# Building the last attention's position bias in the first expert layer's exchange, and writing the attentions' zeros with ScalarE

## The chip, the cores and the metric

The kernel runs on 1 core of one Trainium2 chip. The metric is the device time of one execution in microseconds. The kernel before takes 3750.92 us (median of 3 runs, 3750.13 to 3759.38).

## What is computed

The reference is a stack of four blocks on x of 16 x 64 x 256 (16 sequences of 64 tokens), with a context of 16 x 1601 x 256. Each block is x = x + cross-attention to the context, x = x + self-attention, x = x + feed-forward, each on a layer-normed x. Three pieces matter here.

The last self-attention adds a bias that depends only on the distance of query and key and on the head; nothing in it depends on x:

```python
rel_pos = pos[None, :] - pos[:, None]
buckets = _relative_position_bucket(rel_pos)          # 64 x 64, values 0..31
rel_bias = rel_emb[buckets].transpose(2, 0, 1)[None]  # rel_emb is 32 x 16
att = jnp.einsum('bhqd,bhkd->bhqk', q, k) * (1.0 / math.sqrt(D)) + rel_bias
att = jnp.where(causal[None, None], att, -jnp.inf)
y = jnp.einsum('bhqk,bhkd->bhqd', jax.nn.softmax(att, axis=-1), v)
```

The second block's self-attention is of the same kind without bias and mask. The first block's feed-forward is a mixture of 8 experts: each token goes to 2 of them, each expert takes at most 160 tokens.

## The kernel before

**Order of the work.** x stays in SBUF as 8 tiles of 128 tokens. The stages run one after the other: the first block's attentions (l0_xattn, l0_attn), its experts (l0_ffn), and so on to l3_xattn and l3_attn; l1_attn and l3_attn both call token_attention. The pools decide which memory a tile gets; a tile whose memory belonged to another waits until every use of that other one is over, a DMA's too. The order on each engine follows the program where a helper pins it: mm and tr (L2465, L2470) pin TensorE's, and a Written wrapper (L59) pins what it issues for its engine. Elsewhere the order is the scheduler's. Each engine works strictly in its own order, so an instruction that waits holds all behind it on that engine.

**l0_attn and the exchange.** l0_attn works on two halves a and b of x (4 tiles each). Its last layer's feed-forward for b is feed_last, interleaved with route for each pair of tiles. route (L807 among its lines) computes the gate, ranks the experts, finds with two matmuls (pos) the place of each token in its expert's list, makes put and get from it, and lets GpSimd scatter the tokens to the DRAM tensor taken by four indirect DMAs per pair. route(b, 1) is the last. Then l0_ffn reads the lists back (xs and xw, L947 and L950, on SP's queue, behind the last scatter), TensorE transposes them, VectorE and ScalarE copy the transposes to xsT (L127, L129), and TensorE runs the experts (hidden, out); results go to the DRAM tensor given, and GpSimd gathers them from there (got, L1077). softmax_small (L401 to L406) on the gate's logits, and rms and rr for the next stage (L1095 to L1098), are small VectorE and ScalarE steps that the scheduler puts on VectorE between route(b, 1) and the xsT copies. The tile h1T0, a's hidden layer of l0_attn, is last read by feed's second product for a.

**l3_attn.** It loads its weights, then emb (the 32 x 16 embeddings, four copies on 4 x 32 partitions) and hot (one-hot buckets, 1 MB) by eight DMAs on SP's queue (L2209, L2210). 64 matmuls pb <- emb, hot, which the trace counts as 128, pick the bias (L2215), and 32 VectorE additions (L2225) add the causal mask and lay it out as bias, 128 x 1024.

**token_attention.** Before anything else it makes ones and bq. linear(i) works on half i of the tokens: xln of four tiles on VectorE (L158), transposes on TensorE, two copies to xT, four products of 512 columns (lin_t) of which the first two go to qb by VectorE and ScalarE (L2539, L2540) and the next two to kT, then four products to vm (L2553). Two PSUM buffers serve these products. vm (128 x 4096) holds each value twice, with zeros for the other heads; in linear(0) GpSimd fills it with zeros (L2527). GpSimd also adds the output bias to x there (L2531).

Of the kernel before, what the change touches and what calls it, by code (L numbers as in the profile page):

```python
# [12 lines left out]
F32 = mybir.dt.float32  # L13
I32 = mybir.dt.int32
BF16 = mybir.dt.bfloat16
AF = mybir.ActivationFunctionType
ALU = mybir.AluOpType
# [3 lines left out]
P = 128  # L21
B, S, D = 16, 64, 256
T = B * S
NT = T // P
KC = D // P
# [3 lines left out]
H = 16  # L29
# [35 lines left out]
class Sections:  # L65
# [370 lines left out]
    def l0_attn(self):  # L436
        nc, tc, d = self.nc, self.tc, self.d
# [22 lines left out]
        with ExitStack() as ctx:  # L460
            sb = ctx.enter_context(tc.tile_pool(name="l0a", bufs=1, side="right", reuse_waits="tile"))
            sb2 = ctx.enter_context(tc.tile_pool(name="l0a2", bufs=2, side="right", reuse_waits="tile"))
            ps_kv = ctx.enter_context(tc.tile_pool(name="l0a_kv", bufs=1, space=PSUM, reuse_waits="tile"))
            ps = ctx.enter_context(tc.tile_pool(name="l0a_ps", bufs=1, space=PSUM, reuse_waits="tile"))
            V, A, G = (Written(tc, e) for e in (nc.vector, nc.scalar, nc.gpsimd))
            pieces = self.context_squares(sb2, A)

            def squares(n):
                for _ in range(n):
                    next(pieces, None)  # L470
# [19 lines left out]
            def measure(s, src, p):  # L490

                mv = sb.tile([P, 2, 2], F32, tag=f"ln_mv{s.i}", name="ln_mv", bufs=2)
                for j in range(2):
                    st = sb.tile([P, 6], F32, tag="ln_st", name="ln_st", bufs=3)
                    V.bn_stats(st, src[:, 2 * p + j, :])
                    V.bn_aggr(mv[:, j, :], st)
                r = sb.tile([P, 2], F32, tag=f"ln_r{s.i}", name="ln_r", bufs=2)
                V.tensor_scalar(r, mv[:, :, 1], 1.0, 1e-5, ALU.mult, ALU.add)
                A.activation(r, r, AF.Sqrt)
                s.by[p] = mv, r  # L500

            def norm(s, src, p):

                mv, r = s.by[p]
                V.reciprocal(r, r)
                for j in range(2):
                    t = 2 * p + j
                    V.tensor_scalar(s.n[:, t, :], src[:, t, :], mv[:, j, 0:1], r[:, j : j + 1], ALU.subtract, ALU.mult)
# [190 lines left out]
            def go(it, n=99):  # L699
                for _ in range(n):  # L700
                    if next(it, self) is self:
                        break
# [112 lines left out]
            a, b = Half(0), Half(1)  # L815
# [57 lines left out]
            go(fd)  # L873
            go(fb, 1)

            for s, p in ((a, 0), (a, 1), (b, 0)):
                rt = route(s, p)
                measure(s, s.x, p)
                go(fb, 1)
                norm(s, s.x, p)  # L880
                for n in (1, 1, 1, 1):
                    go(fb, n)
                    go(rt, 1)
                go(fb, 2)
            go(fb)
            measure(b, b.x, 1)
            norm(b, b.x, 1)
            go(route(b, 1))
            squares(999)
            self.pinned = False  # L890

# [1301 lines left out]
    def l3_attn(self):  # L2193
        nc, tc, d = self.nc, self.tc, self.d
        with ExitStack() as ctx:
            sb = ctx.enter_context(tc.tile_pool(name="l3a", bufs=1, reuse_waits="tile"))
            sb2 = ctx.enter_context(tc.tile_pool(name="l3a2", bufs=2, reuse_waits="tile"))
            ps = ctx.enter_context(tc.tile_pool(name="l3a_ps", bufs=1, space=PSUM, reuse_waits="tile"))
            w = self.w8(d["L3_attn_W_attn"], "wqkv")
            wo = self.w2(d["L3_attn_W_proj"], "wo")  # L2200
            rows = self.row(sb, "L3_attn_b_attn", "L3_attn_b_proj")


            emb = sb.tile([P, H], F32, tag="emb", name="emb")
            hot = sb.tile([P, 16, P], F32, tag="hot", name="hot")
            buckets = d["buckets"].rearrange("n (k q) -> n k q", k=S)
            for r in range(4):
                o = slice(32 * r, 32 * r + 32)
                nc.sync.dma_start(emb[o], d["L3_attn_rel_emb"])  # L2209
                nc.sync.dma_start(hot[o], buckets[:, 16 * r : 16 * r + 16, :])  # L2210
            pb = ps.tile([P, 4, 512], F32, tag="sc", name="pb", bufs=1)
            for k in range(16):
                for r in range(4):
                    o = slice(32 * r, 32 * r + 32)
                    nc.tensor.matmul(pb[:, r, k * H : (k + 1) * H], hot[o, k, :], emb[o], start=True, stop=True)  # L2215
            bias = sb.tile([P, 4, 4, S], F32, tag="bias", name="bias")
            above = self.c("above").unsqueeze(1)
            for h in range(2):
                o = slice(h * S, (h + 1) * S)
                for r in range(4):  # L2220
                    keys = slice(16 * r, 16 * r + 16)
                    of = pb[o, r, : 16 * H].rearrange("p (k g r h) -> p h g r k", g=2, r=4, h=2)[:, h]
                    for g in range(KC):
                        for j in range(2):
                            nc.vector.tensor_tensor(  # L2225
                                bias[o, :, 2 * g + j, keys], of[:, g], above[o, :, keys].to_broadcast([S, 4, 16]), ALU.add)
            self.token_attention(
                sb, sb2, ps, w, wo, self.v("L3_attn_b_attn"), rows, 0.25, False, bias, self.l3_ffn(sb, sb2, ps))

# [261 lines left out]
    def token_attention(self, sb, sb2, ps, w, wo, bias_t, rows, scale, own_input, bias=None, then=None):  # L2491
# [4 lines left out]
        nc = self.nc  # L2496
# [5 lines left out]
        vm = sb.tile([P, NT, 2, D], F32, tag="vm", name="vm")  # L2502
# [10 lines left out]
        def linear(i):  # L2513

            x = self.x[:, i * HT : (i + 1) * HT, :]
            xln = sb.tile([P, HT, D], F32, tag=f"xln{i}", name="xln")
            xT = sb.tile([P, KC, 512], F32, tag=f"xT{i}", name="xT")
            for t in range(0, HT, 2):
                pt = ps.tile([P, KC, 2, P], F32, tag="mm", name="tr", bufs=2)
                for j in range(2):  # L2520
                    self.normed(i * HT + t + j, xln[:, t + j, :])
                    for c in range(KC):
                        self.tr(pt[:, c, j, :], xln[:, t + j, c * P : (c + 1) * P], self.ident)
                self.copy(xT[:, :, t * P : (t + 2) * P], pt.rearrange("p c j x -> p c (j x)"))
                yield
            if i == 0:
                nc.gpsimd.memset(vm, 0.0)  # L2527

            if own_input:
                nc.gpsimd.tensor_tensor(x, x, xln, ALU.add)  # L2530
            nc.gpsimd.tensor_tensor(x, x, bo.unsqueeze(1).to_broadcast([P, HT, D]), ALU.add)  # L2531
            for n in range(4):
                pm = ps.tile([P, 512], F32, tag="mm", name="lin_t", bufs=2)
                for k in range(KC):
                    self.mm(pm, w[:, k, n * P : (n + 1) * P], xT[:, k, :], start=(k == 0), stop=(k == KC - 1))
                if n < KC:
                    to = qb[:, n, i * HT : (i + 1) * HT].rearrange("p t j h s -> p (t j) h s")
                    of = pm.rearrange("p (b s) -> p b s", s=S)
                    nc.vector.tensor_scalar(to[:, :, 0, :], of, bias_t[:, n : n + 1], own[:, 0:1], ALU.add, ALU.mult)  # L2539
                    nc.scalar.activation(to[:, :, 1, :], of, AF.Identity, bias=bq[:, n, 1:2], scale=own[:, 1:2])  # L2540
                elif n == KC:
                    nc.vector.tensor_scalar(kT[:, 0, i * 512 : (i + 1) * 512], pm, bias_t[:, n : n + 1], None, ALU.add)
                else:
                    nc.scalar.activation(kT[:, 1, i * 512 : (i + 1) * 512], pm, AF.Identity, bias=bias_t[:, n : n + 1])
                yield
            for t in range(HT):
                pm = ps.tile([P, D], F32, tag="mm", name="lin", bufs=2, padded_shape=[P, 512])
                for k in range(KC):
                    self.mm(pm, xT[:, k, t * P : (t + 1) * P], w[:, k, 2 * D : 3 * D], start=(k == 0), stop=(k == KC - 1))
                of, by = (z.rearrange("p (g h e) -> p g h e", h=2, e=16) for z in (pm, bv))  # L2550
                for h in range(2):
                    to = vm[:, i * HT + t, h].rearrange("p (g h e) -> p g h e", h=2, e=16)
                    nc.vector.tensor_tensor(to[:, :, h], of[:, :, h], by[:, :, h], ALU.add)  # L2553
                yield
# [66 lines left out]
        for _ in linear(0):  # L2621
            pass
        rest = linear(1)
        es, ready = {}, []
        for t in range(NT + 2):
# [205 lines left out]
```

## Time and profile before

| | us |
|---|---|
| median of the runs | 3750.92 |
| lowest and highest run | 3750.13, 3759.38 |
| the profiled execution | 3755.68 |
| its span | 3753.9 |
| busy: TensorE / VectorE / ScalarE / GpSimd | 3443.9 / 1983.8 / 1452.0 / 1292.3 |
| zero fill of vm, GpSimd, each of 2 | 3.51 |
| pb, 128 matmuls | 7.33 |
| bias, 32 additions | 4.55 |
| TensorE's granted clock in the span | 0.957 of full |

All places in time are microseconds from the start of the span of the profiled execution. "Idle before, released by" at an instruction means that its engine had nothing to do before it, and what ended that. A line of the timeline merges equal instructions that follow each other (x6 is six of them), and its duration is then from the start of the first to the end of the last. Starts of neighbouring VectorE instructions can overlap by about 0.1 us. TensorE's busy time is modelled; the granted clock is what the throttle allowed, as a share of full speed.

### The profile page before, as it was taken

To read this page: it belongs to the slowest core of one execution; us is meant where nothing else is said; L and a number is where in the kernel's file an instruction comes from. 1 tells how busy PE (TensorE), PEld (TensorE's weight loads), DVE (VectorE), ACT (ScalarE), POOL (GpSimd) and SP (SyncE) were. 2 spreads that over 40 slices of the span, in tenths; PEclk is the share of its full clock that TensorE was granted. 3 is DMA by queue.
4 is the path that set the end of the run, shared out by engine and by line. 5 is a ranking of instruction groups with operands and counts; after the bars stand their busy time and mean duration, and the time that the engine had idled before them with its cause. 6 is when DMAs were issued, how large, how long until landed. Compare 5 with 4: busy or idle time off the path is not lost.

```text
span 3753.9 us, 70772 instructions
## 1 busy us (share of the span) xinstructions
PE 3443.9 (92%) x30951; PEld 2189.3 (58%) x30966; DVE 1983.8 (53%) x3682; ACT 1452.0 (39%) x2079; POOL 1292.3 (34%) x787
## 2 busy tenths in 40 slices
PE   8999999996999968999978998999999789999986
PEld 4555555563655644555545666667676555555454
DVE  5343333436555545656657554667767655333346
ACT  2333333343444423444423433466666512111223
POOL 1555555552011123333321001577777530000012
PEclk9999999998999979999988999999999879999986
DMA  4111001101332344342101001111111004111740
GB/s 145 38 38 38 26 31 38 38 10 35 103 95 88 108 165 147 139 146 107 40 27 40 1 6 63 50 56 38 56 38 38 11 2 174 41 35 33 299 159 13
DMA packets 106123, 258.66 MB, mean 69 GB/s; under 512 B 9203, under 2 KB 74483, under 8 KB 103510
## 3 DMA queue, kind: packets, MB, share of 16 engines
q1 hardware_dynamic: 97366, 222.68, 16.7%
q10 hardware_dynamic: 6912, 27.27, 2.4%
q8 instruction: 243, 3.98, 0.4%
q0 software_dynamic: 1536, 4.20, 0.4%
q14 instruction: 66, 0.54, 0.0%
HBM read 248.34 MB, written 5.77 MB: 68 GB/s over the span
## 4 chain that ended last, share of the span: by engine, by line
PE 76%; DVE 13%; ACT 7%; issue 3%; POOL 1%; DMA 0%; another core or an unknown queue 0%; SPq 0%; ACTq 0%; DVEq 0%; POOLq 0%
PE sc L2465 15%; PE pk L2465 15%; PE lin L2465 7%; PE acc L2465 6%; PE lin_t L2465 5%; ACT e L349 4%; PE pu L2465 4%; PE gate L2035 3%; PE up L2035 3%; PE lin L216 3%; PE pc L1658 3%; PE prz L2465 2%; PE turn L2470 2%; PE gelu_t L1575 2%; PE pa L2465 1%
## 5 line engine op out<-in xcount | busy, mean ns | idle before, releaser
L2398 POOL TENSOR_TENSOR tot<-tot,e 128x1024 f32<-128x1024 f32 (+1 forms) x340 | 803.4, 2363 | 374.9 <-ACT e L349 252.1
L292 DVE TENSOR_REDUCE m<-sc 128x4 f32<-128x2048 f32 x96 | 220.1, 2293 | 272.7 <-PE sc L2465 271.6
L1802 DVE SCALAR_TENSOR_TENSOR e<-sc,row_L_xattn_nbias,free 128x2048 f32<-128x2048 f32 x104 | 244.3, 2349 | 115.6 <-PE sc L2465 114.0
L1804 ACT ACTIVATE e<-e 128x2048 f32<-128x2048 f32 x104 | 198.7, 1910 | 246.1 <-DVE e L1802 246.1
L349 ACT ACTIVATE e<-sc 128x2048 f32<-128x2048 f32 x104 | 195.2, 1877 | 241.4 <-PE sc L2465 237.3
L2465 PE MATMUL sc<-qb,kT 32*128 32x128 f32 x6656 | 245.6, 284 | 38.2 <-DVE m L306 12.3
L2465 PEld LDWEIGHTS sc<-qb,kT 32*128 32x128 f32 x6656 | 206.7, 187 | 82.3 <-issue 24.1
L2465 PE MATMUL acc<-e,v 128*32 128x128 f32 x6656 | 226.6, 276 | 6.4 <-ACT e L1805 6.4
L2465 PEld LDWEIGHTS acc<-e,v 128*32 128x32 f32 x6656 | 170.2, 110 | 106.0 <-issue 95.2
L2465 PE MATMUL pk<-cT,wk 128*128 128x512 f32 (+1 forms) x512 | 208.2, 536 | 3.6 <-DVE rows L322 3.6
L2465 PE MATMUL pk<-wv,cT 128*128 128x256 f32 x832 | 209.8, 394 | 0.0
L1805 ACT ACTIVATE e<-e 128x2048 f32<-128x2048 f32 x104 | 198.7, 1911 | 3.2
L2465 PE MATMUL pk<-wkv,cT 128*128 128x256 f32 x832 | 196.3, 386 | 0.0
L2465 PE MATMUL pk<-cT,wkv 128*128 128x512 f32 (+1 forms) x512 | 194.9, 522 | 0.0
L2465 PEld LDWEIGHTS pk<-wv,cT 128*128 128x128 f32 x832 | 149.5, 190 | 75.7 <-issue 58.2
L2465 PEld LDWEIGHTS pk<-wkv,cT 128*128 128x128 f32 x832 | 153.2, 190 | 28.5 <-issue 4.3
L1658 PE MATMUL pc<-ew,eh 128*128 128x256 f32 x640 | 158.0, 389 | 0.0
L2465 PE MATMUL pu<-cn,e 128*64 128x257 f32 (+1 forms) x1248 | 145.1, 389 | 12.8 <-POOL e L1210 12.8
L2465 PE MATMUL sc<-kT,qb 32*128 32x512 f32 (+2 forms) x1536 | 140.7, 465 | 14.9 <-DVE m L292 2.3
L2039 ACT ACTIVATE g<-gate 128x512 f32<-128x512 f32 x68 | 40.6, 597 | 293.3 <-PE gate L2035 293.2
L1200 POOL TENSOR_TENSOR e<-e,mx 128x512 f32<-128x512 f32 x96 | 81.9, 885 | 193.2 <-DVE mx L1199 193.2
L2465 PE MATMUL sc<-cT,qT 128*64 128x512 f32 (+1 forms) x768 | 141.9, 522 | 3.6 <-ACT scs L1180 3.1
(515 smaller groups left out, 6265.6 us busy)
## 6 DMA issues: line engine op xcount, KB each, us to landing
cT<-in_ctx_t SPq DMA_DIRECT2D x128, 832.0 KB
cn<-in_ctx_n SPq DMA_DIRECT2D x32, 1664.0 KB
piece<-in_ctx_n ACTq DMA_DIRECT2D x32, 640.0 KB
w<-in_L_attn_W SPq DMA_DIRECT2D x8, 1024.0 KB
piece<-in_ctx_n ACTq DMA_DIRECT2D x16, 384.0 KB
w<-in_L_ffn_W SPq DMA_DIRECT2D x16, 256.0 KB
down<-in_L_ffn_w_down SPq DMA_DIRECT2D x16, 256.0 KB
gate<-in_L_ffn_w_gate SPq DMA_DIRECT2D x16, 256.0 KB
```

The lines of the kernel that those rows point to most:

```text
L216: nc.tensor.matmul(pm, xT[:, k, t * P : (t + 1) * P], w[:, k, :], start=(k == 0), stop=(k == kc - 1))
L292: nc.vector.tensor_reduce(x.m4[:, g, :, i], pm, AX.X, ALU.max)
L349: nc.scalar.activation(e, pm, AF.Exp, scale=0.25)
L1200: pin(nc.gpsimd.tensor_tensor(p.e, p.e, p.mx.unsqueeze(2).to_broadcast(p.shape), ALU.subtract))
L1575: nc.tensor.matmul(pm, w[:, c, lo : lo + m], cT[:, c, :], start=(c == 0), stop=(c == nk - 1))
L1658: nc.tensor.matmul(pc[:, n, j, :], s.eh[i][:, c, tok], ew2[:, c, cols], start=False, stop=(c == 3))
L1802: nc.vector.scalar_tensor_tensor(e16, pm16, nb, free[:, at : at + P].unsqueeze(1).to_broadcast([P, 16, P]), ALU.add, ALU.mult)
L1804: nc.scalar.activation(e, e, AF.Relu)
L1805: nc.scalar.activation(e, e, AF.Square)
L2035: nc.tensor.matmul(pm[-1], w[:, k, n * P : (n + 1) * P], xT[:, k, tok], start=(k == 0), stop=(k == KC - 1))
L2398: nc.gpsimd.tensor_tensor(tot[:w], x.first if c == 1 else tot[:w], e[:w], ALU.add)
L2465: ins = self.nc.tensor.matmul(*args, **kw)
```

## The change

It does two things. The bias of the last attention is built in l0_attn, behind route(b, 1), and written to a DRAM tensor, position_bias; l3_attn loads it by one DMA of 512 KB. Its inputs are loaded into a tile named kept, which takes the memory of h1T0, ahead of the four route calls; kept holds the one-hot buckets, the embeddings and the bias. The matmuls go to four PSUM banks of l0_attn's own pools, pinned in TensorE's order behind pos; the additions are pinned in VectorE's order behind get; the write to DRAM is issued on GpSimd's queue. The zeros of vm are written by a pinned ScalarE activation, Identity with scale 0 of a broadcast constant, instead of GpSimd's fill, in both attentions.

```diff
 def l0_attn(self):
             go(fb, 1)
+            kept = sb.tile([P, 8, 512], F32, tag="h1T0", name="kept").rearrange("p a b -> p (a b)")
+            hot = kept[:, : 16 * P].rearrange("p (k q) -> p k q", q=P)
+            emb = kept[:, 16 * P : 16 * P + H]
+            bias = kept[:, 24 * P : 24 * P + 16 * S].rearrange("p (r g s) -> p r g s", r=4, g=4)
+            buckets = d["buckets"].rearrange("n (k q) -> n k q", k=S)
+            for r in range(4):
+                o = slice(32 * r, 32 * r + 32)
+                nc.sync.dma_start(emb[o], d["L3_attn_rel_emb"])
+                nc.sync.dma_start(hot[o], buckets[:, 16 * r : 16 * r + 16, :])
             for s, p in ((a, 0), (a, 1), (b, 0)):
                 rt = route(s, p)
...
             go(route(b, 1))
+            banks = ps_kv.tile([P, 2, 512], F32, tag="kv", name="pb")
+            banks = [banks[:, 0], banks[:, 1], *(ps.tile([P, 512], F32, tag="tr", name="pb", bufs=2) for _ in range(2))]
+            for k in range(16):
+                for r in range(4):
+                    o = slice(32 * r, 32 * r + 32)
+                    self.mm(banks[r][:, k * H : (k + 1) * H], hot[o, k, :], emb[o], start=True, stop=True)
+            above = self.c("above").unsqueeze(1)
+            for h in range(2):
+                o = slice(h * S, (h + 1) * S)
+                for r in range(4):
+                    keys = slice(16 * r, 16 * r + 16)
+                    of = banks[r][o, : 16 * H].rearrange("p (k g r h) -> p h g r k", g=2, r=4, h=2)[:, h]
+                    for g in range(KC):
+                        for j in range(2):
+                            V.tensor_tensor(
+                                bias[o, :, 2 * g + j, keys], of[:, g], above[o, :, keys].to_broadcast([S, 4, 16]), ALU.add)
+            self.position_bias = tc.dram_tile([P, 16 * S], F32, name="position_bias")
+            nc.gpsimd.dma_start(self.position_bias, bias.rearrange("p r g s -> p (r g s)"))
             squares(999)
 def l3_attn(self):
-            emb, hot: two tiles and eight loads
-            pb: 64 matmuls
             bias = sb.tile([P, 4, 4, S], F32, tag="bias", name="bias")
-            32 additions into bias
+            nc.sync.dma_start(bias.rearrange("p r g s -> p (r g s)"), self.position_bias)
 def token_attention(...), in linear(0):
-                nc.gpsimd.memset(vm, 0.0)
+                Written(self.tc, nc.scalar).activation(
+                    vm.rearrange("p t h (a x) -> p (t h a) x", x=P), self.ident.unsqueeze(1).to_broadcast([P, NT * 2 * KC, P]),
+                    AF.Identity, scale=0.0)
```

In the order of the changed program the first VectorE instruction behind the additions is sm_mx of softmax_small; its memory is part of what kept held, and it waits for the kept tile's loads and for the write to position_bias.

More of the change, by code (lines that the diff above doesn't have):

```diff
@@ L2201, in l3_attn @@
             rows = self.row(sb, "L3_attn_b_attn", "L3_attn_b_proj")
[L2204 to L2215, printed above, removed]
-            bias = sb.tile([P, 4, 4, S], F32, tag="bias", name="bias")
[L2217 to L2226, printed above, removed]
+            bias = sb.tile([P, 4, 4, S], F32, tag="bias", name="bias")
+            nc.sync.dma_start(bias.rearrange("p r g s -> p (r g s)"), self.position_bias)
             self.token_attention(
```

## The prediction

> **What bounds the kernel now.** I read the chain of work that ended last first, then the timeline of the three places that the change touches, then windows for the granted clock. The chain:
>
> ```profile
> PE 76%; DVE 13%; ACT 7%; issue 3%; POOL 1%; DMA 0%; another core or an unknown queue 0%; SPq 0%; ACTq 0%; DVEq 0%; POOLq 0%
> ```
>
> TensorE carries three quarters of it, but the change works where TensorE is idle or runs something small, so shares don't price it; each place has to be followed. First the start of the last attention:
>
> ```profile
> 3614.77 3.51 POOL L2527 MEMSET vm<- 128x4096 f32 x1
> 3615.10 3.26 DVE L2510 TENSOR_TENSOR bq<-vecs,cst 128x4 f32<-128x4 f32 x1
> 3615.18 6.96 DVE L158 TENSOR_SCALAR xln<-x,xm,xr 128x256 f32<-128x256 f32 x6
> 3616.06 1.13 PE L2465 MATMUL lin<-wv,hT 128*128 128x256 f32 x4 [0.52 <-ACT hT L2159]
> 3619.54 2.44 POOL L2531 TENSOR_TENSOR x<-x,row_L_attn_b_attn 128x1024 f32<-128x1024 f32 x1 [0.97 <-DVE xln L158]
> 3622.05 0.41 DVE L380 TENSOR_TENSOR x<-lin,x 128x256 f32<-128x256 f32 x1
> 3622.52 7.33 PE L2215 MATMUL pb<-emb,hot 32*128 32x16 f32 x128 [5.33 <-DVE x L380]
> 3629.88 4.55 DVE L2225 TENSOR_TENSOR bias<-pb,cst 64x64 f32<-64x64 f32 x32 [4.99 <-PE pb L2215]
> 3634.46 0.69 DVE L127 COPY xT<-tr 128x512 f32<-128x512 f32 x1
> 3635.30 8.99 PE L2465 MATMUL lin_t<-xT,wqkv 128*128 128x512 f32 x16 [3.56 <-DVE xT L127]
> 3639.76 0.78 ACT L2540 ACTIVATE qb<-lin_t,bq,cst 128x512 f32<-128x512 f32 x1 [7.39 <-DVE qb L2539]
> ```
>
> Columns: start, duration, instruction, idle time before it and who ended it. bq is 4 columns and took 3.26 us (0.14 in the other attention): VectorE stood still until GpSimd's zero fill of vm ended at 3618.28. Of the six xln, the last stood until GpSimd's addition ended at 3621.98; VectorE and GpSimd exclude each other here. VectorE's copies out of PSUM don't suffer. Then pb (7.33) and bias (4.55) follow in the chain, and xT waits behind both. Next the first expert layer's exchange:
>
> ```profile
> 1353.64 0.59 PE L2465 MATMUL pos<-count,cst 128*128 128x16 f32 x2
> 1355.59 0.21 DVE L401 TENSOR_REDUCE sm_mx<-logits 128x8 f32<-128x64 f32 x1
> 1359.68 0.96 POOL L807 DMA_INDIRECT taken<-n,put  x1 [0.31 <-issue]
> 1362.22 0.38 SPq L947 DMA_DIRECT2D xs<-taken  x1
> 1366.23 0.42 DVE L127 COPY xsT<-tr 128x256 f32<-128x256 f32 x1 [7.23 <-DMA xw<-taken]
> 1368.11 2.50 PE L2465 MATMUL hidden<-xsT,w 128*128 128x160 f32 x8 [0.52 <-DVE xsT L127]
> ```
>
> TensorE idles from 1354.23 to 1365.08, VectorE from 1359.0 to 1366.23, while the tokens go out to DRAM and back. From 1368.11 TensorE is busy without a gap. Last, the zero fill in the other attention:
>
> ```profile
> 1920.77 3.51 POOL L2527 MEMSET vm<- 128x4096 f32 x1
> 1921.18 3.34 DVE L158 TENSOR_SCALAR xln<-x,xm,xr 128x256 f32<-128x256 f32 x1
> 1924.58 1.97 PE L2470 MATMUL tr<-cst,xln 128*128 128x128 f32 x8 [7.27 <-DVE xln L158]
> ```
>
> The same block: one xln of 0.38 us took 3.34, and the transposes waited for it.
>
> **Last attention: minus 14.7 us.** In the changed order the transposes stand right behind lin of the last tile and need only xln. Without the fill, identb, bq and four xln (0.29 us each, the pace of 3618.36 to 3619.54) run from 3615.05 to 3616.6. TensorE transposes from 3617.2 to 3618.3 (full clock, 1.09 us as at 3648.95). GpSimd's addition takes 3616.6 to 3619.05 and holds the sixth xln. Then VectorE does L380, the two statistics (0.42, 0.42, 0.18) and, in its new order, its copy of xT (0.69): ready at 3620.9 instead of 3635.15. Now the new zeros decide. They are one ScalarE activation of 128x4096, put ahead of qb in its queue and behind the root of xr, which waits for VectorE. No row has that size; 1024 columns take 1.06 us and 2048 take 1.91, so 0.83 ns a column: 3.6 us. It runs from about 3621.3 to 3624.95. Behind it stands qb of the first product; TensorE has two product buffers and its third product waits for that qb. The first product (3.44 us at half clock, as at 3635.3) is out at 3624.4, VectorE's qb at 3625.2, ScalarE's at 3626.0. The third product starts there instead of at 3640.59: 14.6 to 14.7 us. The zeros are thus almost hidden by product and qb; were the clock full, they would be the bound at the same 3625.8. The rest of the stage is unchanged. Bounds: 12.3 (VectorE held by GpSimd's second addition, 2.4 us, before qb) to 15.5 (the 0.8 us by which qb follows the zeros gone). The eight loads at 3590 to 3604 become one of 512 KB, long before its use at 3649: nothing.
>
> **Other attention: minus 2.4 us.** The held xln ends at 1921.65 instead of 1924.52: 2.87. But GpSimd's two additions now run back to back (2.44 and 2.35 us) and can hold the later xln until 1927.65; with 1.1 us of VectorE work behind, qb comes at 1928.4 to 1928.9 where the product would allow 1928.17. ScalarE's zeros (1924.35 to 1928.0) are hidden under the first product, cover 0.2 us; without it each us costs one. 2.87 less 0.2 to 0.75; bounds 1 to 3.
>
> **Exchange: plus 6.6 us.** Added are eight loads, 128 matmuls, 32 additions and a write. The loads wait on SP's queue until h1T0 is free, after the product that ends at 1286.8; SP had nothing else to issue until 1331.98, and 1 MB is in long before 1354: nothing. The matmuls stand behind pos, at 1354.25. Their row is pb. One rule speaks for less: the Trainium skill's "TensorE: Matmul & The Clock Gate", Part 1 (the HAM clock gate), lets the clock double after about 3.4 us of sustained work. By it, 59 of the matmuls at 57 ns and 69 at half of that: 5.4 us. But the row shows the 128 at 358 to 387 ns each from first to last, and the windows show
>
> ```profile
> 3622.00:3626.00 4.00, 3.48 (x64) 3.48 (x66) 2.48 (x9) 0.20 (x1) 1.37 (x1) 0.50 0.02 4
> 3626.00:3630.00 4.00, 4.00 (x72) 3.96 (x71) 0.12 (x1) 0.00 (x0) 1.09 (x1) 0.50 0.00 0
> ```
>
> clock 0.50 (third last column) throughout; it is 0.50 from 1346 to 1365 too. I take 7.33: pb ends at 1361.6. The additions (4.55) end at 1366.1, in VectorE's order right behind get. So far the cover holds: xw lands at 1366.4.
>
> The write is where it fails. In the changed program sm_mx, VectorE's next instruction, takes memory of the kept tile and waits until the write to DRAM has landed. Behind sm_mx on VectorE stand the softmax, rms and rr, and then the xsT copies that TensorE's hidden needs. The write is issued by GpSimd behind the puts (over at 1360.64), so at 1366.1. No direct write from GpSimd is in the trace. Nearest is the last put: 128 KB landed 2.39 us after its issue. 384 KB more at the 245 to 316 GB/s of the busy windows is 1.2 to 1.6 us: 3.8, and 0.2 for what is left of the xs loads: 4.0. The skill's "DMA: Bandwidth & Descriptors", Anatomy of one DMA, gives 2.0 us and bytes at 436 GB/s: 3.2. Above: the gather got at 1399.06 took 5.67 for 128 KB in the chain, with the DMA engines full. I take 4.0: landed at 1370.1. Then the softmax chain, 3.45 us (1355.59 to 1359.0, with ScalarE's table load in it), and the two xsT copies: hidden starts at 1374.4 instead of 1368.11, 6.3. TensorE has idled longer, 0.3 for a colder start. As TensorE is gapless after it and SP issues the next stage's loads behind the results, all of it stays. Bounds: 2.8 (full clock, see the first rival) to 10.1 (the gather's 7.5 us to its consumer).
>
> **Sum.** Minus 14.7, minus 2.4, plus 6.6: minus 10.5. The profiled execution (3755.68, span 3753.9) becomes 3745.2; the runs' median lies 4.8 lower, at 3750.92, and becomes 3740.4. That is 0.28%; 0.3% (11.3 us), about what a measurement of this kernel can tell from no change, is just not reached.
>
> **Rivals.** First, a cheaper exchange: the matmuls warm up, or the write lands sooner. At full clock pb takes 3.7 us, hidden starts at 1370.8, cost 2.8: sum minus 14.3, 3736.6. By both rules: cost 6.6 less 1.9 less 0.8, minus 13.2. For it speaks the rule, against it the row. Second, a dearer one: the write under load as slow as the gather to its consumer (1394.01 to 1401.53, 7.5 us) costs 3.5 more, or the zeros on ScalarE take 5 us and delay both qb by about 1.5: minus 7, 3744. Against it: DMA share is only 0.24 from 1368 to 1371. Third, slower than before: the software queue's write moves bytes at the gather's rate, 5.67 us for each 128 KB, so 22.7 for 512. VectorE would wait until 1388.8, cost 25.3: sum plus 8.2, 3759. It decides from 14.5 us for the write. Against it speaks the put. Fourth, a change that does nothing can't be: pb and the fill both stand in the chain.
>
> **Chances.** The likeliest case (minus 8 to minus 12.5) 0.62, a third of it beyond 0.3%; cheaper 0.16; dearer 0.17; slower 0.05, half of it beyond 0.3%. Faster 0.37, within 0.59, slower 0.04. The range reaches from the cheap exchange (3735.5) to the dear one with some spread of the runs (3748.5).
>
> **What would show it.** pb at 1354 for 7.3 us at clock 0.5; sm_mx some 14.5 us later than before, released by the write; hidden about 6.5 us after its old place; bq and xln short in both attentions; an activation vm of about 3.6 us, and qb right behind it; the last attention's third product 14.7 us earlier against the stage's start. Wrong if sm_mx doesn't wait for the write, if pb warms, or if VectorE is held elsewhere by GpSimd.

## The result, and the profile after

The changed kernel takes 3744.42 us (median of 21 runs, 3738.89 to 3757.99), the kernel before beside it 3753.40 (21 runs, 3747.72 to 3763.49). The ratio is 0.9982, 95% interval 0.9976 to 0.9988: 0.18% faster, within 0.3%. Two more groups of runs gave 0.9968 (0.9957 to 0.998) and 0.9979 (0.997 to 0.9988); by medians the three gains are 9.0, 11.2 and 8.1 us. The predicted 3740.4 lies 4.0 below the measured median; 2.5 of that is the reference, since the kernel before has a median of 3753.40 in 21 runs where the prediction had 3750.92 from three. The profiled execution takes 3741.89 us, span 3740.1.

The last attention, by the timeline of the changed kernel (columns as before):

```profile
3618.68 0.16 DVE L2517 TENSOR_TENSOR bq<-vecs,cst 128x4 f32<-128x4 f32 x1
3618.75 4.06 DVE L158 TENSOR_SCALAR xln<-x,xm,xr 128x256 f32<-128x256 f32 x6
...
3623.74 0.66 DVE L127 COPY xT<-tr 128x512 f32<-128x512 f32 x1
...
3624.55 3.67 PE L2472 MATMUL lin_t<-xT,wqkv 128*128 128x512 f32 x8 [2.90 <-DVE xr L153]
3624.68 3.62 ACT L59 ACTIVATE vm<-cst 128x4096 f32<-128x4096 f32 x1
...
3628.20 1.68 ACT L2549 ACTIVATE qb<-lin_t,bq,cst 128x512 f32<-128x512 f32 x2
...
3629.01 3.70 PE L2472 MATMUL lin_t<-xT,wqkv 128*128 128x512 f32 x8 [0.80 <-ACT qb L2549]
```

bq is back to 0.16 us, pb and bias are gone, and the products start right behind xT. Here the first two products ran at full clock (8 matmuls in 3.67 us), so TensorE had both out while ScalarE still wrote zeros (3624.68 to 3628.30). The third product waited for the qb behind them: "0.80 <-ACT qb".

The exchange, by the timeline of the same execution:

```profile
1351.93 0.59 PE L2472 MATMUL pos<-count,cst 128*128 128x16 f32 x2
1352.45 5.30 PE L2472 MATMUL pb<-kept 32*128 32x16 f32 x92
...
1358.46 0.92 PE L2472 MATMUL pb<-kept 32*128 32x16 f32 x5 [0.71 <-issue]
1359.93 1.92 PE L2472 MATMUL pb<-kept 32*128 32x16 f32 x31 [0.54 <-issue]
...
1361.86 4.55 DVE L59 TENSOR_TENSOR kept<-pb,cst 64x64 f32<-64x64 f32 x32 [7.89 <-PE pb L2472]
...
1366.71 0.59 POOL L918 DMA_DIRECT2D position_bias<-kept  x1 [7.78 <-DVE kept L59]
1369.73 0.22 DVE L401 TENSOR_REDUCE sm_mx<-logits 128x8 f32<-128x64 f32 x1 [3.32 <-issue]
...
1374.07 2.50 PE L2472 MATMUL hidden<-xsT,w 128*128 128x160 f32 x8 [6.75 <-DVE xsT L127]
```

The chain is the predicted one: pb, additions, write, sm_mx, the softmax, xsT, hidden. "issue" at sm_mx means that the profile names no releaser; in the program it is the write, and in e6 below the profile names it. pb itself stalled in this execution, and took 9.4 us instead of 7.33: the two gaps shown are 1.25 us of that, the rest is spread over shorter ones.

The other attention: TensorE's transposes stand there as

```profile
1929.79 1.97 PE L2477 MATMUL tr<-cst,xln 128*128 128x128 f32 x8 [4.34 <-DVE xln L158]
...
1932.28 3.62 ACT L59 ACTIVATE vm<-cst 128x4096 f32<-128x4096 f32 x1
```

with 4.34 us of idle time ahead of them, where it was 7.27.

Executions drift against each other by some us from place to place, so absolute starts don't compare. I use three distances within a place: from the second pair of pos matmuls to the first hidden; the idle time ahead of the other attention's first transposes, plus the time from those to the first scores (sc); and from the last tile's transposes of h to the last attention's first scores. In us, each good to about 0.02:

| kernel | pos to hidden | idle + tr to sc | h to last sc |
|---|---|---|---|
| before, before again (e8) | 14.47, 14.60 | 23.23, 23.15 | 32.79, 33.38 |
| after, again (e7), third (e10) | 22.14, 21.52, 21.23 | 20.08, 20.03, 20.05 | 17.65, 17.64, 18.53 |
| e1 zeros only | 14.40 | 20.12 | 30.22 |
| e2 bias only | 21.25 | 23.18 | 16.84 |
| e3 softmax ahead | 16.56 | 20.11 | 17.64 |
| e4 pb early | 15.12 | 20.22 | 18.54 |
| e5, e9 pb early, fill kept | 15.38, 15.23 | 20.01, 20.30 | 16.85, 18.53 |
| e6 write by ScalarE | 24.03 | 20.04 | 17.65 |

Against the first row's first execution the three of the changed kernel give plus 6.8 to 7.7, minus 3.15 to 3.2, and minus 14.3 to 15.15: sums of minus 10.6, 11.3 and 10.7. Against e8, the second execution of before, the last attention gains 0.6 more and the sums are minus 11.3, 11.9 and 11.3. Predicted was minus 10.5, or minus 10.8 without the 0.3 us that the prediction added behind hidden, where these distances do not reach.

### The profile page after: what moved, and what is told of

Read it like the earlier page. It is cut to its first block, busy times and chain, and to the rows that moved or that the text cites. A ratio compares the mean times of both kernels' runs of the same rounds, so it can differ in the third digit from the quotient of the medians.

```text
span 3740.1 us, 70775 instructions
## 1 busy us (share of the span) xinstructions
PE 3434.1 (92%) x30951; PEld 2183.0 (58%) x30966; DVE 1975.9 (53%) x3682; ACT 1459.0 (39%) x2081; POOL 1284.7 (34%) x786
## 4 chain that ended last, share of the span: by engine, by line
PE 49%; DVE 8%; ACT 3%; issue 2%; POOL 0%; DMA 0%; another core or an unknown queue 0%; SPq 0%; DVEq 0%; POOLq 0%; ACTq 0%
PE pk L2472 9%; PE sc L2472 8%; PE pu L2472 4%; PE acc L2472 3%; PE gate L2065 3%; PE up L2065 3%; PE lin L216 3%; PE pc L1688 3%; PE prz L2472 2%; PE gelu_t L1605 2%; PE turn L2477 2%; PE lin L2472 1%; PE pa L2472 1%; PE pn L2472 1%; DVE e L1832 1%
```

## Experiments

**e1 and e2: each part alone.**

```diff
 e1: before.py
-                nc.gpsimd.memset(vm, 0.0)
+                Written(self.tc, nc.scalar).activation(
+                    vm.rearrange("p t h (a x) -> p (t h a) x", x=P), self.ident.unsqueeze(1).to_broadcast([P, NT * 2 * KC, P]),
+                    AF.Identity, scale=0.0)
 e2: the changed kernel
-                Written(self.tc, nc.scalar).activation(
...
+                nc.gpsimd.memset(vm, 0.0)
```

> Only the zeros of vm move to ScalarE; the bias stays in the last attention. My account of the traces: 2.6 us gained in the other attention, and in the last one about what bq and the sixth xln lost to the fill, 2.6 us, since pb follows there as before and hides the zeros: minus 5.2 us in all (ratio 0.9986). Rival, that the last attention's whole gain comes from the zeros: minus 15 us. Rival, that ScalarE's zeros only move the wait: 0.

> Only the bias moves; GpSimd keeps filling vm. Gain in the last attention about 11.5 us (pb and its additions, 11.9, less what the fill still holds). My account of the changed kernel's trace, which has 9.9 us of cost between pos and the second block: net minus 1.6 us (ratio 0.9996). The prediction's own figure for the exchange, 6.6: net minus 5 us (0.9987). Which of the two shows whether the extra 3.3 us are the change's or that one execution's.

e1: 3747.23 us against 3752.63, ratio 0.9984 (0.9973 to 0.9995). By the table minus 3.1 in the other attention and minus 2.6 in the last, 5.7 where the account had 5.2: it holds, and both rivals fall. e2: 3745.06, ratio 0.9983 (0.9971 to 0.9994). Its exchange costs 6.8 us, with pb in 7.03 us and no stall. So the prediction's figure for the exchange was the right one, and the 9.9 us which I had read off the first pair of traces held run-to-run drift. But the last attention gained 15.95 us where I had expected 11.5. The timeline of e2 shows why:

```profile
3606.51 0.15 POOL L2513 MEMSET ones<- 128x64 f32 x1 [22.07 <-PE pa L2472]
3606.67 3.51 POOL L2534 MEMSET vm<- 128x4096 f32 x1
...
3617.44 0.15 DVE L2517 TENSOR_TENSOR bq<-vecs,cst 128x4 f32<-128x4 f32 x1
```

The fill ran a tile earlier, over 7 us ahead of bq, and held nobody. GpSimd waits for a pa product before `ones`, and the fill stands right behind `ones`; in before it waits for the last tile's pa, to 3614.59, here for the one before it. `ones` comes a tile early in every run that moves the bias and not in e1. That the memory of emb and hot, now free, is the reason is inferred from how the pools work; no run shows it. So in the last attention the two parts of the change undo each other: the zeros on ScalarE are worth 2.6 us while the bias is built there, and minus 0.8 once it is gone (17.65 against 16.84), at full clock.

**e3: the wait for the write taken off VectorE's way.**

```diff
-            self.softmax_small(sb, probs, E)
-            keep = sb.tile([P, E], F32, tag="keep", name="keep")
+            self.softmax_small(self.routed, probs, E)
+            keep = self.routed.tile([P, E], F32, tag="keep", name="keep")
```

> The changed kernel with the softmax's two small tiles in a pool that lives longer, so that no VectorE instruction ahead of the xsT copies waits for the write of position_bias; the scheduler then puts the softmax ahead of the additions, and rms and rr stay behind them. If the write and the chain behind it are the exchange's main cost: hidden starts 4.3 us earlier than in the changed kernel, and the ratio to before falls from 0.9982 to about 0.9970. If pb and the additions are the cost and the write is not: at most 1 us, 0.998.

3738.87 us, ratio 0.9963 (0.9951 to 0.9976). hidden comes 16.56 us behind pos, 4.7 to 5.6 sooner than in the changed kernel; pb and additions are unchanged. Of the exchange's 7 us the write and the softmax behind it are thus about 5; the additions with rms and rr behind them, and a last 0.5 us that the profile puts down to the loads of xs, are 2.1. The write's wait with the softmax behind it is the main cost; the rival falls.

**e4: pb where TensorE is warm and idle.**

```diff
             go(fb)
+            banks = ps_kv.tile([P, 2, 512], F32, tag="kv", name="pb")
+            banks = [banks[:, 0], banks[:, 1], ps.tile([P, 512], F32, tag="po", name="pb"), ps.tile([P, 512], F32, tag="mm", name="pb", bufs=3)]
+            for k in range(16):
...
             measure(b, b.x, 1)
             norm(b, b.x, 1)
             go(route(b, 1))
-            banks = ps_kv.tile([P, 2, 512], F32, tag="kv", name="pb")
...
```

> The changed kernel with pb and its additions moved ahead of the last pair's normalisation, to where TensorE has just finished feed_last and idles for 5 us; pb uses four banks that are free there. If pb is at full clock there: 3.7 us, hidden; the additions take VectorE 4.55 us. If the scheduler's order puts them on the path to the last route, its cost moves to the puts, up to 4.55 us plus what is left of pb; if VectorE's wait there is short, the exchange costs 4 to 6 us instead of 9.9. Ratio to before 0.9966 to 0.9972. It also shows whether pb stalls when no put is in flight: no stall by the theory that the puts' traffic holds TensorE's instructions, stalls after some 92 matmuls if it is the number of instructions.

The expectation has the additions move too; in the kernel that ran they stayed behind get, so its case of additions on the path to the last route doesn't apply. 3738.10 us, ratio 0.996 (0.9945 to 0.9974). Timeline and window of e4 (second column of the window after its width: TensorE; 1.00 is the granted clock, then DMA share and GB/s):

```profile
1339.33 3.76 PE L2472 MATMUL pb<-kept 32*128 32x16 f32 x128
...
1359.79 0.59 POOL L918 DMA_DIRECT2D position_bias<-kept  x1
...
1362.85 0.22 DVE L401 TENSOR_REDUCE sm_mx<-logits 128x8 f32<-128x64 f32 x1 [3.58 <-issue]
...
1367.91 2.50 PE L2472 MATMUL hidden<-xsT,w 128*128 128x160 f32 x8 [0.52 <-DVE xsT L127]
```

```profile
1339.00:1343.00 4.00, 4.00 (x130) 3.66 (x128) 3.12 (x10) 0.20 (x1) 2.88 (x3) 1.00 0.87 288
```

pb takes half the time and is hidden; the additions and the write run while the tokens travel, and sm_mx, though it still waits for the write, does so early enough. The exchange costs 0.65 us. pb ran while four puts were issued and DMA share was 0.87, without a stall: the theory that the puts' traffic holds TensorE's instructions has nothing for it here.

**e5 and e9: e4 with the last attention's fill back on GpSimd.**

```diff
             if i == 0:
-                Written(self.tc, nc.scalar).activation(
...
+                if own_input:
+                    Written(self.tc, nc.scalar).activation(
...
+                else:
+                    nc.gpsimd.memset(vm, 0.0)
```

> The kernel of e4 (bias moved, its matmuls behind feed_last) with ScalarE's zeros in the other attention only; in the last attention GpSimd fills vm again. In e2 that fill began 11 us ahead of the last attention's start, since without emb and hot the memory of vm came free earlier, and it held nobody. If so here: minus 3.1 in the other attention, minus 16 in the last, exchange within 0.7 of before: minus 18.4 us, ratio 0.9951, 0.8 to 1.7 us better than e4 in the last attention. If the fill falls back to its old place: bq takes 3.3 us again and the last attention gains 12 to 13; ratio 0.996 to 0.9965.

> The kernel of e5 once more, on one chip with the changed kernel, since e5's interval (0.995 to 0.9978) holds both the full gain and the changed kernel's own. If the traces' terms add up (minus 3.1, minus 16, plus 0.9): minus 18 us, ratio 0.9951, and 7 us below the changed kernel. If the gain is eaten up elsewhere: no more than 3 us below it.

e5: 3740.07 us, ratio 0.9964 (0.995 to 0.9978); e9: 3735.79 us, ratio 0.9959 (0.9945 to 0.9972), and on the same chip the changed kernel (e10) 3743.50, 0.9979 (0.997 to 0.9988). e9 is 7.7 us below it by medians, about what the exchange had cost; of all kernels run it has the lowest median. The early fill came again in both. In e5 the last attention takes 16.85, as in e2; in e9 18.53, as in e4 and e10, because there the first product ran at half clock, which hides ScalarE's zeros as well. So this piece is worth 0.8 us or nothing, and by their times e3, e4, e5 and e9 are not told from each other.

**e6: the write on ScalarE's queue.**

```diff
-            nc.gpsimd.dma_start(self.position_bias, ...)
             squares(999)
+            nc.scalar.dma_start(self.position_bias, ...)
```

> The changed kernel with the write of position_bias issued on ScalarE's queue, behind its last squares, instead of GpSimd's. If GpSimd's part in the write (its instruction takes 0.59 us, and the write took 3.0 us there in one execution and 4.5 in another) is what VectorE waits for: sm_mx comes 0.5 to 1.5 us sooner after the additions, ratio about 0.9979. If it is the 512 KB that take the time: no change, 0.9982.

3747.33 us, ratio 0.9991 (0.998 to 1.0001), and hidden 9.6 us late, by neither theory. The timeline:

```profile
1365.60 0.34 ACTq L919 DMA_DIRECT2D position_bias<-kept  x1
1368.29 0.88 SPq L968 DMA_DIRECT2D w<-in_L_ffn_W  x2
1368.44 0.22 DVE L401 TENSOR_REDUCE sm_mx<-logits 128x8 f32<-128x64 f32 x1 [2.88 <-DMA position_bias<-kept]
...
1371.45 0.38 SPq L977 DMA_DIRECT2D xs<-taken  x1
```

sm_mx did come 2.9 us behind the additions. But the loads of xs were issued at 1371.45, over 9 us late against pos. On SP's queue they stand behind two weight loads (w) and b2w, and in that program the first of these two counts its completion on the same semaphore as the write, so it waits for the write to land. It was issued at 1368.29, and xs behind it. So the experiment shows the write alone at 2.84 us, and does not tell what GpSimd's queue costs in the exchange.

**e7, e8 and e10: the two kernels again.**

> The changed kernel once more, for a second execution's profile. If the two stalls within pb (2 us in all) and the late arrival of the second gather (0.8 us) are that execution's: pb in 7.0 to 7.3 us without a stall, hidden 6.3 to 6.8 us after its old place. If they are the change's: they come again, hidden 7.7 us late.

> The kernel before once more, for a second execution's profile. Between hidden and the second block's middle (1392 to 1480) the kernels e1 to e4 gained 1.6 to 3.5 us on the first profile of before, e1 too, in which nothing is changed there. If that is the first execution's bad luck, this one is about 3 us shorter there.

> The changed kernel beside it. By the terms of the traces (minus 15.15 in the last attention, minus 3.1 in the other, plus 6.8 to 7.1 in the exchange) minus 11.2 us, ratio 0.9970; by its first measurement 0.9982. Its profile shows the exchange a third time: the write's wait between 3.3 and 5.1 us after the additions, hidden 6.8 to 7.7 us late.

e7: 3738.30 us, ratio 0.9968; e8: 3748.85 us in one run. Timeline of e7:

```profile
1351.68 7.03 PE L2472 MATMUL pb<-kept 32*128 32x16 f32 x128
1358.74 4.55 DVE L59 TENSOR_TENSOR kept<-pb,cst 64x64 f32<-64x64 f32 x32 [5.53 <-PE pb L2472]
...
1363.59 0.59 POOL L918 DMA_DIRECT2D position_bias<-kept  x1 [5.43 <-DVE kept L59]
1368.36 0.22 DVE L401 TENSOR_REDUCE sm_mx<-logits 128x8 f32<-128x64 f32 x1 [5.07 <-issue]
```

pb without a stall, in e10 as well: the stalls were that one execution's. In return the write took longer here, 4.77 us from its issue to sm_mx (e2: 4.50, e10: 4.48) against 3.02. The windows around the write, first of after, then of e7 (last two columns: DMA share, GB/s):

```profile
1366.00:1370.00 4.00, 1.32 (x7) 0.92 (x5) 0.63 (x4) 0.00 (x0) 0.59 (x1) 0.50 0.51 189
```

```profile
1364.00:1368.00 4.00, 1.09 (x4) 0.72 (x4) 0.00 (x0) 0.00 (x0) 0.18 (x1) 0.50 0.86 308
```

In e7 the write meets the last loads of xs, issued from 1362.09 on; in after the stalls had made it late enough to travel alone. In e4, e5 and e9, where it is issued ahead of these loads, it took 3.06 to 3.07. That the loads lengthen it is read from this overlap; no run took them away. Of the 2.4 us that pb had lost, after got 1.75 back this way. e8 needed 3.9 us less between 1392 and 1480 than the first execution of before, with the same program, so the 9.9 us held that execution's own delay.

## Why the prediction was right

**Place and sign.** The steps were seen: pb at half clock behind pos, additions, sm_mx behind the write, hidden late; bq and xln short; qb right behind the zeros in after and e7, though not in e10. The sum, minus 10.5 against minus 10.6 to 11.9, was right to 1.5 us. That is in part luck: the exchange came out dearer and the attentions, but for the last one in one execution, better than predicted, and these errors offset each other. The 0.3 us for a colder start can't be told from drift.

**Last attention, predicted 14.7, measured 14.3 to 15.15 (14.85 to 15.75 against e8).** The zeros take 3.62 us, predicted 3.6. Whether they or the product bind depends on the clock of the first product, half in e10 and full in after and e7; the prediction had both at the same place, and they are 0.9 apart. What it did not see: it charged the 3.3 us at bq to the fill where it stood. With the bias gone the fill would have moved ahead by itself (e2), so ScalarE's zeros earn nothing here. Nor was bq itself what the fill held. In the other attention of before it ran in the midst of the fill (1920.77 to 1924.28), at its usual pace:

```profile
1921.12 0.14 DVE L2510 TENSOR_TENSOR bq<-vecs,cst 128x4 f32<-128x4 f32 x1
```

In the last attention the cast identb stands ahead of bq in VectorE's order; it took 3.39 us with the fill and 0.22 without, and bq ended with it. The prediction's "VectorE and GpSimd exclude each other" is thus too wide: the cast and xln were held by the fill, bq was not. The sum is the same.

**Other attention, predicted 2.4, measured 3.15 to 3.2.** The failed term is "less 0.2 to 0.75" for xln held by GpSimd's additions. The additions ended where it said, 6.0 us behind the start of the transposes; but only 0.5 us of VectorE work stood between them and qb, where it had 1.1. The last xln ended at 1936.27, and qb followed the first product's start by 3.82 us, as in before: the hold just fits into the cover.

**Exchange, predicted 6.3 to hidden, measured 6.8 to 7.7 (6.6 to 7.5 against e8).** Three terms were off and partly cancel. pb: 7.03 instead of 7.33, or 9.4 with the stalls. The write: predicted 4.0, measured 3.0 alone and 4.5 to 4.8 with the xs loads. The prediction gave the loads 0.2 us; by the overlap they cost 1.5 to 1.75, and the write alone was 0.8 quicker than the put suggested, close to the 3.2 us estimated from the Trainium skill's "DMA: Bandwidth & Descriptors", Anatomy of one DMA. And 0.3 us between the last addition and GpSimd's issue had no term. Behind sm_mx all was as predicted: 4.3 us to hidden.

**The rule weighed.** The skill's "TensorE: Matmul & The Clock Gate", Part 1, spoke for pb warming after 3.4 us. In the exchange the clock stayed at 0.50 in all six executions in which pb ran there, through 7 to 9 us. For these small matmuls the rule did not hold; what would count as sustained work was not tested. Behind feed_last, with TensorE warm, pb took 3.76 us at 1.00 (e4, e5, e9). The first rival's 3.7 us was thus a true figure for another place.

**What stays open.** The first measurement's interval, 4.5 to 9.0 us, ends short of the sum; the third's reaches to 11.3 us, and the second's has it in its middle. Some 2 us may go elsewhere. The executions themselves differ by more, and most of that goes with TensorE's clock. Of the 24 runs of before beside e5 to e8, the 6 with a granted clock of 0.957 or 0.958 have a median of 3758.28 us, the 11 with 0.961 or 0.962 one of 3747.80. The traces say the same: from the other attention's first scores to the last tile's transposes of h, where the change only puts one load for eight, the twelve executions took 1673.1 to 1686.8 us, with the clock at half for 106 to 143 us of it, and the longer ones are those with more time at half (correlation 0.92). Why the clock stands at half longer in one execution than in the next is open, and so is whether the change moves it outside the three places.

Stalls that the profile puts down to "issue" hit TensorE's acc matmuls in different spots each time, such as this in the other attention in e1 (its timeline for TensorE):

```profile
1968.11 0.46 PE L2465 MATMUL acc<-eT,ones 64*32 64x64 f32 x32 [1.85 <-issue]
```

Over acc they add up to 0.7 to 5.3 us an execution (the longest is 2.63, in e4), with no order by kernel (before 0.7 and 2.8, the changed kernel 1.5, 3.1 and 1.3). What causes them, and those in pb, was not found.

## What to carry to other kernels

A wait for DMA is cover for an engine only if nothing that stands behind the added work in that engine's order is due when the wait ends: here memory reuse alone chained the softmax, and the experts behind it, to a write whose result nobody needed for 2200 us. Put the small steps that are due first into memory of their own, and the matmuls where TensorE is still warm. When one edit removes tiles, look again at where the pools let other instructions start; the second edit may then be paid for a problem that has left.

## What was not expected of the hardware

128 matmuls of 32x16, back to back, did not raise TensorE's clock from 0.50 in 7 to 9 us, but ran at 1.00 when started directly behind full-size matmuls. A 512 KB write to DRAM from GpSimd's queue held its waiter for 3.0 us with the DMA engines half free (share 0.51) and 4.8 with them busy (0.86). GpSimd's fill held a VectorE cast of 128x128 (3.39 us against 0.22) and a tensor_scalar of 128x256 (3.34 against 0.38), but not a product of two SBUF operands of 128x4 (0.14). TensorE stalled for up to 2.63 us within dense runs of small matmuls, at places that changed from one execution to the next.
